# Last values after the last sums in the attention; the last image's 3x3 convolution by pairs of rows

## The chip, the cores and the metric

One core of a Trainium2 chip runs the whole program. The metric is the time of one execution on the device in microseconds, the median of several runs. All data are 32-bit floats.

## The reference

Four images of 128 channels and 64 x 64 pixels go through four layers. Each layer normalises its input by groups of channels, applies something, and adds the result to the input.

```python
# x: (4, 128, 64, 64)
x = x + attention(gn(x))      # layer 0: 4096 x 4096 scores for each image
x = x + conv5x5(gn(x))        # layer 1: weights built from radial tables
x = x + selective_scan(gn(x)) # layer 2: 64 + 64 channels, 64 states, both directions
x = x + conv3x3(gn(x)) + b    # layer 3

def attention(x):             # per image, n = 4096 pixels
    q, k, v = xt @ Wq.T + bq, xt @ Wk.T + bk, xt @ Wv.T + bv
    return softmax(q @ k.T * C ** -0.5) @ v

def conv2d(x, w, b):          # layer 3: 3x3, padding 1, with w of (128, 128, 3, 3)
    y = conv_general_dilated(x, w, (1, 1), [(1, 1), (1, 1)], ("NCHW", "OIHW", "NCHW"))
    return y + b[None, :, None, None]
```

## The kernel before, in words

The 128 channels lie on the 128 partitions, and the 4096 pixels of an image along the free dimension. TensorE (PE in the profile) works on blocks of 512 pixels (`MM`, one PSUM bank); the scan on chunks of 1024 (`CH`).

Two streams of work are written as Python generators and interleaved by hand, and the order in which they are emitted is the order in which each engine executes. One stream is `scan_core`, the recurrence of layer 2: 256 ticks for each image, in each of which GpSimd (POOL) multiplies `db<-dx,br` (L1082), ScalarE (ACT) makes decays `da` (L1075), VectorE (DVE) runs the recurrence (L1092) and part of the weighing (L1095), POOL the other part (L1113), and PE collects `y<-hc,sel` (L1127). The other stream, `images()`, is all the rest: for each image the attention, the 5x5 convolution and the operands of the scan (`front`), and later the end of layer 2 and the 3x3 convolution (`scan_end`, `back`). The scan of image b runs beside the front of image b+1. Every `yield` of the second stream states an estimate of its PE time (`PRODUCT` 0.86 us for a product of 512 columns, `HOP` 1.7 us), and after each half tick of the scan the program takes as many steps of the second stream as a credit of 2.8 us for a tick (`PACE`) allows; it is 1.5 us (`ENDPACE`) once no front is left. Before an image's first tick, `before(b)` takes steps of the second stream until the scan's operands of that image have been emitted. For image 0's front there is no scan yet, and after the last image's scan nothing but its own `scan_end` and `back` remains.

**The attention** of an image has 8 blocks of 512 queries, each with 32 tiles of 128 keys, so 256 units `u`. In unit u PE makes the scores (`sc`, L465), ACT the exponentials (`pt`, L471) into a ring of 8 slots, and PE adds `values(u - 2)` into the bank `acc` (L477). The sums of exponentials are made on PE from four ring slots at a time (`zp`, L499) in images 1 to 3. In image 0 (`fill`) DVE and POOL add them in `sided` and `sidep` (`side_sums`, L519). At the end of a block `evict` copies `zp` and `acc` out with ACT (`zs` L525, `raw` L527), `turn` turns the sums by tiny products (`pz`, L539), `invert` takes their reciprocals on DVE (L548, L550), `widen_out` spreads these with PE (`pzb`, L457), and `settle` multiplies and adds the residual on DVE (L562, L563). For blocks 0 to 6 these steps are spread over the next block's units. For block 7 they follow one another directly, after all of the block's values. Then the group norm of the 5x5 convolution waits for the last of the results.

**The 3x3 convolution** (`conv`, called from `back`) copies the normalised image into a padded tile `xpm` with ACT in four pieces (L370), and makes 8 blocks of 9 accumulated products each (`pcm`, L644). PE reads 32-bit floats in two records for each product in the trace, so 72 products are 144 records. For images 0 to 2 it runs beside the scan. For image 3 it is the last work of the program: DVE adds bias and residual straight from PSUM (L1278), and SP sends 256 KB to HBM (L1279). After it come the check of the range of the sums (`out_of_range`, L1396), its load into registers and a branch around a second, careful version of the program (`safe`), which is not taken with these inputs.

Of the kernel before, what the change touches and what calls it, by code (L numbers as in the profile page):

```python
# [24 lines left out]
F32 = mybir.dt.float32  # L25
# [27 lines left out]
def conv_preact_kernel(  # L53
# [170 lines left out]
    taps5 = cw[:, :NTAP, :]  # L224

    m3 = cw[:, : main_w.shape[1], :]
    kept = dram.tile([P, main_w.shape[1], C], F32, tag="kept", bufs=1, name="kept")

    def build_conv_weights(tmp):
        xx_sb = tmp.tile([P, NTAP, C], F32, name="xx_sb")  # L230
        nc.sync.dma_start(xx_sb, xhat)
        id_sb = tmp.tile([P, C], F32, name="id_sb")
        nc.sync.dma_start(id_sb, identity)
        picked = tmp.tile([P, 2, NTAP, C // 2], F32, name="picked")
        for n, (which, table, inds) in enumerate((("xx", wxx, indsxx), ("id", wid, indsid))):
            nr, oc = table.shape[1], table.shape[2]
            acc = picked[:, n]
            one = cw.rearrange("p k c -> p (k c)")[:, : NTAP * oc]
            one = one.rearrange("p (k o) -> p k o", o=oc)
            tab = tmp.tile([P, nr, oc], F32, name=f"tab{which}")  # L240
            nc.sync.dma_start(tab, table)
            ii = tmp.tile([P, NTAP], I32, name=f"ii{which}")
            nc.sync.dma_start(ii, inds.to_broadcast([P, NTAP]))
            fi = tmp.tile([P, NTAP], F32, name=f"fi{which}")
            nc.vector.tensor_copy(fi, ii)

            ng = tmp.tile([P, NTAP], F32, name=f"ng{which}")
            nc.vector.tensor_scalar(ng, fi, 0.0, float(nr), ALU.is_lt, ALU.mult)
            nc.vector.tensor_tensor(fi, fi, ng, ALU.add)
            nc.vector.tensor_scalar(fi, fi, 0.0, float(nr - 1), ALU.max, ALU.min)  # L250
            for r in range(nr):
# [26 lines left out]
        nc.sync.dma_start(kept, m3)  # L278

# [140 lines left out]
    def attention(b, xs, xn, v, st, safe, loads):  # L420
# [97 lines left out]
                s = sides[blk, e]  # L518
                eng.tensor_tensor(s, s, ring[:, u % NRING, :], ALU.add)  # L519

        def evict(blk):
# [47 lines left out]
        queries(0)  # L569
        ready.add((b, "begun"))  # L570
        yield HOP
        for u in range(N + 2):
            blk, j = divmod(u, NJT)
            cost = sums_due(u)
            if u < N:
                if safe and j == 0:
                    row_max(blk)
                scores(u)
                cost += PRODUCT
            w = u - 2  # L580
            if 0 <= w < N:
                values(w)
                cost += PRODUCT
# [8 lines left out]
                if d == NJT - 1:  # L592
                    evict(blk - 1)
                    if blk < NM:
                        for n, f in ((1, turn), (2, invert), (4, widen_out), (5, settle)):
                            after(u, n, f, blk - 1)
                    else:
                        turn(blk - 1)
                        invert(blk - 1)
                        yield PRODUCT  # L600
                        widen_out(blk - 1)
                        settle(blk - 1)
                        ready.add((b, "attended"))
                        break
            if j == 17 and blk + 1 < NM:
                queries(blk + 1)
                cost += PRODUCT
            for f, args in later.pop(u, ()):
                f(*args)
                cost += PRODUCT if f in (turn, widen_out) else 0.0  # L610
            next(loads, None)
            yield cost or HOP


    def conv(b, xs, tag, st, weights, k, finish, name, residual=False):
# [40 lines left out]
            done = i, acc  # L656
        yield HOP
        finish(*done)

# [539 lines left out]
    def program(safe):  # L1199
# [1 line left out]
        mats4, ynds, ends = {}, {}, {}  # L1201
        ready.clear()
        if safe:
            nc.sync.dma_start(m3, kept)

        def load(tile, b):
            for c in range(NCH):
# [15 lines left out]
        def front(b, xn, v):  # L1223
# [19 lines left out]
            if b + 1 < B:  # L1243
                return (yield from both(operands, start(b + 1, 10)))
            yield from operands

        def stage(b, pieces, done):

# [19 lines left out]
        def back(b):  # L1268
            xs, st, _ = ends[b]

            def put(i, acc):
                cut = bass.ts(i, MM)
                if b + 1 < B:
                    to = pools["bg"].tile([P, MM], F32, tag="w", bufs=4, name=f"o_{b}_{i}")
                    nc.scalar.activation(to, acc, AF.Identity, bias=col(MAINB))
                else:
                    to = xs[:, cut]
                    nc.vector.scalar_tensor_tensor(to, acc, col(MAINB), to, ALU.add, ALU.add)  # L1278
# [180 lines left out]
```

## Time and profile before

| | |
|---|---|
| median of 3 runs | 4513.8 us (4513.7, 4513.8, 4527.3) |
| profiled execution | 4519.1 us, of which the span on the engines is 4517.3 us |
| PE busy | 3996.2 us, 88% of the span |
| DVE busy | 3667.9 us, 81% |
| POOL busy | 3638.5 us, 81% |
| ACT busy | 2399.5 us, 53% |
| image 0's attention on PE | from 28 to 505 us |
| fronts of images 1, 2, 3 on PE | about 700 to 1670, 1660 to 2640, 2620 to 3580 us |
| last image's 3x3 convolution on PE | 4444.0 to 4508.7 us |

A busy share is an average over stages with different limits. PE is busy for 98 to 100 in each 100 us of the attentions that run beside a scan, and DVE and POOL are at 92 to 99 in the stage after 3700 us, where only the scan and short convolutions remain. At both ends of the program, image 0's front and the last convolution, one stream alone is running. Times in a view are counted from the start of the span.

### The profile page before, as it was taken

What the parts mean: (1) busy time and instruction counts of PE and PEld (TensorE: products, weight loads), DVE (VectorE), ACT (ScalarE), POOL (GpSimd) and SP (SyncE); (2) the same over time, 40 slices, a digit from 0 to 9 for tenths busy, and PEclk for the clock granted to TensorE, in tenths of its full rate; (3) what the DMA queues carried; (4) which work ended last, traced back from release to release, by engine and by line L of the source; (5) the groups of instructions that cost most, each with busy time, mean ns of one, the idle gap of its engine ahead of it and who ended that gap; (6) DMA issues with size and microseconds to landing.
All of it is one profiled execution on the core that took longest, in us unless ns stands there. A gap on an engine that the chain in (4) does not pass through costs nothing. (4 is left out here: it accounts for less than half of the span.)

```text
span 4517.3 us, 43608 instructions
## 1 busy us (share of the span) xinstructions
PE 3996.2 (88%) x13528; PEld 1482.2 (33%) x13528; DVE 3667.9 (81%) x3643; ACT 2399.5 (53%) x4420; POOL 3638.5 (81%) x1731
## 2 busy tenths in 40 slices
PE   8999998999999979999999879999999658575767
PEld 4444433333333323333333223333333112121212
DVE  4721217999998978999989879999999799999992
ACT  3333227666664476666654566666654654544441
POOL 3433308999998969999989789999999899999992
PEclk9999999999999989999999989999999878697888
DMA  1000016445444565455445555455445565656561
GB/s 63 6 1 1 5 60 229 171 168 180 170 175 157 174 218 196 172 179 174 174 154 177 188 209 176 162 176 177 175 161 182 211 226 203 233 193 231 184 233 48
DMA packets 210582, 719.51 MB, mean 159 GB/s; under 512 B 24864, under 2 KB 25760, under 8 KB 210208
## 3 DMA queue, kind: packets, MB, share of 16 engines
q1 hardware_dynamic: 208736, 715.87, 44.8%
q8 instruction: 109, 1.79, 0.2%
q14 instruction: 137, 1.12, 0.1%
q10 hardware_dynamic: 1600, 0.73, 0.1%
HBM read 649.07 MB, written 67.44 MB: 159 GB/s over the span
## 5 line engine op out<-in xcount | busy, mean ns | idle before, releaser
L1082 POOL TENSOR_TENSOR db<-dx,br 128x1024 f32<-128x1024 f32 x1024 | 2400.0, 2367 | 226.9 <-DMA dx<-dxd 76.7
L1075 ACT ACTIVATE da<-de,a_neg 128x512 f32<-128x512 f32 (+1 forms) x1795 | 1342.1, 751 | 736.0 <-DVE da L1092 444.5
L465 PE MATMUL sc<-r,x 128*128 128x512 f32 x2048 | 1082.5, 611 | 18.3 <-ACT r L434 12.4
L477 PE MATMUL acc<-pt,v 128*128 128x512 f32 x2048 | 1046.5, 593 | 1.6
L1113 POOL TENSOR_TENSOR hc<-hc,cr 128x1024 f32<-128x1024 f32 x406 | 960.1, 2365 | 17.6 <-ACT last L1108 15.1
L471 ACT ACTIVATE pt<-sc 128x512 f32<-128x512 f32 x1024 | 604.4, 590 | 572.4 <-PE sc L465 563.9
L1127 PE MATMUL y<-hc,sel 128*32 128x512 f32 x4096 | 654.2, 650 | 276.6 <-POOL hc L1113 273.5
L1095 DVE TENSOR_TENSOR hc<-da,cr 128x512 f32<-128x512 f32 (+1 forms) x1067 | 828.4, 776 | 68.8 <-issue 1.3
L1092 DVE TENSOR_TENSOR_SCAN da<-da,last,db 128x512 f32<-128x512 f32 (+1 forms) x464 | 728.1, 1569 | 24.1 <-POOL db L1082 17.6
L1092 DVE TENSOR_TENSOR_SCAN da<-da,da,db 128x512 f32<-128x512 f32 x449 | 577.9, 1287 | 14.3 <-ACT da L1075 13.4
L465 PEld LDWEIGHTS sc<-r,x 128*128 128x128 f32 x2048 | 359.1, 190 | 605.0 <-issue 378.4
L477 PEld LDWEIGHTS acc<-pt,v 128*128 128x128 f32 x2048 | 387.5, 190 | 497.2 <-issue 477.9
L1092 DVE TENSOR_TENSOR_SCAN hc<-da,hc,db 128x512 f32<-128x512 f32 x322 | 413.2, 1283 | 61.9 <-ACT da L1075 31.6
L1092 DVE TENSOR_TENSOR_SCAN hc<-da,last,db 128x512 f32<-128x512 f32 (+1 forms) x304 | 455.9, 1500 | 8.4 <-ACT da L1075 4.7
L519 POOL TENSOR_TENSOR sidep<-sidep,pt 128x512 f32<-128x512 f32 x120 | 170.5, 1421 | 279.9 <-ACT pt L471 277.8
L1127 PEld LDWEIGHTS y<-hc,sel 128*32 128x32 f32 x4096 | 94.1, 111 | 732.3 <-POOL hc L1113 363.6
L644 PE MATMUL pcm<-xpm,cw 128*128 128x512 f32 x576 | 291.2, 653 | 30.5 <-ACT xpm L370 30.5
L519 DVE TENSOR_TENSOR sided<-sided,pt 128x512 f32<-128x512 f32 x120 | 96.0, 800 | 227.5 <-ACT pt L471 226.1
L1092 DVE TENSOR_TENSOR_SCAN da<-da,db 128x512 f32<-128x512 f32 (+1 forms) x154 | 231.0, 1500 | 30.9 <-ACT da L1075 16.2
L808 PE MATMUL pe<-df,cw 128*128 128x512 f32 x560 | 255.2, 598 | 0.0
L499 PE MATMUL zp<-pt,ones 128*32 128x512 f32 x1536 | 202.4, 595 | 5.0 <-DVE xs L563 5.0
L1108 ACT COPY last<-da 128x1 f32<-128x1 f32 x469 | 73.1, 156 | 244.3 <-DVE hc L1095 242.5
(209 smaller groups left out, 2743.2 us busy)
## 6 DMA issues: line engine op xcount, KB each, us to landing
br<-bm SPq DMA_DIRECT2D x512, 512.0 KB, 5.2
cr<-cm SPq DMA_DIRECT2D x512, 512.0 KB, 3.9
de<-dd SPq DMA_DIRECT2D x64, 512.0 KB, 4.8
dx<-dxd SPq DMA_DIRECT2D x64, 512.0 KB, 6.2
x<-in_x_dram SPq DMA_DIRECT2D x16, 512.0 KB, 4.6
xs<-in_x_dram SPq DMA_DIRECT2D x16, 512.0 KB, 5.8
xsd<-xs SPq DMA_DIRECT2D x16, 512.0 KB, 5.2
xcd<-xc SPq DMA_DIRECT2D x16, 512.0 KB, 2.7
```

The lines of the kernel that those rows point to most:

```text
L465: nc.tensor.matmul(sc, xn[:, bass.ts(j, P)], rq[blk], start=True, stop=True)
L471: nc.scalar.activation(pt, sc, AF.Exp)
L477: nc.tensor.matmul(acc[blk], v[:, j, :], ring[:, u % NRING, :], start=j == 0, stop=j == NJT - 1)
L519: eng.tensor_tensor(s, s, ring[:, u % NRING, :], ALU.add)
L644: nc.tensor.matmul(acc.rearrange("p (r w) -> p r w", w=W), weights[:, t, :], xp[:, y : y + RPM, dx : dx + W], start=t == 0, stop=t == k * ...
L808: nc.tensor.matmul(flat(acc), cw[:, w * K5 + dx, :] if w < HSUM else more[:, w - HSUM, dx, :], view(r, dx), start=k == 1, stop=k == total ...
L1075: nc.scalar.activation(da, rep["de", b, c, d, g][:, bass.ts(h, size)], AF.Exp, scale=a_neg[:, at(i)])
L1082: nc.gpsimd.tensor_tensor(dbs[i], rep["dx", b, c, d, g], rows["b", b, c, d, q], ALU.mult)
L1092: nc.vector.tensor_tensor_scan(h, da, db[:, cut], before, ALU.mult, ALU.add)
L1095: nc.vector.tensor_tensor(hc[:, cut], h, rows["c", b, c, d, q][:, cut], ALU.mult)
L1113: nc.gpsimd.tensor_tensor(hcs[i], hcs[i], rows["c", b, c, d, q], ALU.mult)
L1127: nc.tensor.matmul(y[r : r + SG, :], sel, hcs[i - KG + 1 + gg][:, bass.ts(h, MM)], start=q == 0, stop=False, tile_position=(0, r), skip_gr ...
```

## The change

1. **Attention, last block of each image.** The values of the last four key tiles (`HELD`) are no longer issued inside the unit loop. After the loop come: values 252, what is pending of the sums, the last sums, the copy `zs` (images 1 to 3), values 253, `turn`, values 254, `invert`, values 255, `widen_out`, the copy `raw`, `settle`. `evict` is split in `evict_sums` and `evict`. In image 0 the last two side sums are issued right after the loop. The number of products is the same.
2. **3x3 convolution of the last image** (`conv_last`). Two output rows are made together from four input rows d0 to d3 and the three rows of weights w0 to w2. The four products are (w0 - w1 + w2)/2 on d2 - d1, (w0 + w1 + w2)/2 on d1 + d2, w0 on d0 - d2, and w2 on d3 - d1. The first output row is the sum of the first three, the second row is the second minus the first plus the fourth. Each of the four takes three products (dx = 1, 0, 2), so 12 for 1024 pixels where there were 18. POOL makes the two combinations with a minus sign on d1 (`cb` tiles from the scan's pool `hc`), DVE the other two. ACT copies the first product out, POOL adds it to and subtracts it from the residual rows, and DVE adds the other products and the bias. The tile `xpl` has no side columns; the outer dx products write 63 of the 64 columns.
3. **Banks.** Chunks 0 and 2 use the two double banks of the scan's decays (`da`); chunks 1 and 3 four single banks (`s`, `a`, `z`, `y`).
4. **Weights and output.** `last_weights` builds six combined rows of weights on DVE after the operands of image 3. The copy `kept` holds 15 taps instead of 9 (983 KB instead of 590 KB). The output leaves in 4 transfers of 512 KB instead of 8 of 256 KB.

```diff
+        def evict_sums(blk):
             zs = None
             if not fill:
                 zs = pools["bg"].tile([P, MM], F32, tag="zs", bufs=1, name=f"zs_{b}_{blk}")
                 nc.scalar.copy(zs, zp.pop(blk))
+            state[blk] = None, zs
+
+        def evict(blk):
             raw = pools["bg"].tile([P, MM], F32, tag="raw", bufs=1, name=f"raw_{b}_{blk}")
             nc.scalar.copy(raw, acc.pop(blk))
-            state[blk] = raw, zs
+            state[blk] = raw, state[blk][1]
...
-        for u in range(N + 2):
+        HELD = 4
+        for u in range(N):
...
-            if 0 <= w < N:
-                values(w)
-                cost += PRODUCT
+            if w >= 0:
+                if w < N - HELD:
+                    values(w)
+                    cost += PRODUCT
...
-                    if blk < NM:
-                        for n, f in ((1, turn), (2, invert), (4, widen_out), (5, settle)):
-                            after(u, n, f, blk - 1)
-                    else:
-                        turn(blk - 1)
-                        invert(blk - 1)
-                        yield PRODUCT
-                        widen_out(blk - 1)
-                        settle(blk - 1)
-                        ready.add((b, "attended"))
-                        break
+                    for n, f in ((1, turn), (2, invert), (4, widen_out), (5, settle)):
+                        after(u, n, f, blk - 1)
...
+        for w in (N - 2, N - 1) if fill else ():
+            side_sums(w)
+        blk = NM - 1
+        values(N - 4)
+        yield PRODUCT
+        while due:
+            sums(due.pop(0)[0])
+            yield PRODUCT
+        if not fill:
+            sums(N - 1)
+            yield PRODUCT
+        evict_sums(blk)
+        values(N - 3)
+        yield PRODUCT
+        turn(blk)
+        values(N - 2)
+        yield PRODUCT
+        invert(blk)
+        values(N - 1)
+        widen_out(blk)
+        evict(blk)
+        yield PRODUCT
+        settle(blk)
+        ready.add((b, "attended"))
...
+    def last_weights():
+        half, above = cw[:, LSUM : LSUM + 3, :], cw[:, LDIF : LDIF + 3, :]
+        nc.vector.tensor_tensor(half, m3[:, 0:3, :], m3[:, 6:9, :], ALU.add)
+        nc.vector.tensor_scalar(half, half, 0.5, None, ALU.mult)
+        nc.vector.scalar_tensor_tensor(above, m3[:, 3:6, :], -0.5, half, ALU.mult, ALU.add)
+        nc.vector.scalar_tensor_tensor(half, m3[:, 3:6, :], 0.5, half, ALU.mult, ALU.add)
+
+    def conv_last(b, xs, st, finish):
+        CK = CH // W // 2
...
+        def piece(c):
+            h0, h1 = 2 * CK * c + (c > 0), min(2 * CK * (c + 1) + 1, H)
+            normalise(rows[:, 1 + h0 : 1 + h1, :], xh[:, h0:h1, :], gn)
...
+        def combine(c):
+            d = [rows[:, 2 * CK * c + k : 2 * CK * (c + 1) + k - 1 : 2, :] for k in range(4)]
+            made = []
+            for eng, pairs in (
+                (nc.gpsimd, ((2, 1, ALU.subtract), (3, 1, ALU.subtract))),
+                (nc.vector, ((1, 2, ALU.add), (0, 2, ALU.subtract))),
+            ):
+                two = pools["hc"].tile([P, CH], F32, tag="hc", name=f"cb_{b}_{c}_{len(made)}")
+                for n, (i, j, op) in enumerate(pairs):
+                    made.append(flat(two[:, bass.ts(n, MM)]))
+                    eng.tensor_tensor(made[-1], d[i], d[j], op)
+            combined[c] = made
+
+        def banks_of(c):
+            if c % 2:
+                return [bank(tag, f"pl{tag}_{b}_{c}") for tag in "sazy"]
+            two = [
+                pools["wide"].tile([P, CH], F32, tag="da", bufs=2, name=f"pl{n}_{b}_{c}")
+                for n in range(2)
+            ]
+            return [t[:, bass.ts(h, MM)] for t in two for h in range(2)]
+
+        def products(acc, view, w):
+            for n, dx in enumerate((1, 0, 2)):
+                to = slice(max(1 - dx, 0), W - max(dx - 1, 0))
+                of_ = slice(max(dx - 1, 0), W - max(1 - dx, 0))
+                nc.tensor.matmul(
+                    flat(acc)[:, :, to], cw[:, w + dx, :], view[:, :, of_],
+                    start=n == 0, stop=n == 2, skip_group_check=True,
+                )
...
+        piece(0)
+        combine(0)
+        piece(1)
+        combine(1)
+        for c in range(NCH):
+            t_, o_, s_, e_ = banks_of(c)
+            diff, odd, total, even = combined.pop(c)
+            products(t_, diff, LDIF)
+            products(s_, total, LSUM)
+            products(e_, even, 0)
+            products(o_, odd, 6)
+            if c + 2 < NCH:
+                piece(c + 2)
+                combine(c + 2)
+            ts_ = pools["bg"].tile([P, MM], F32, tag="w", bufs=4, name=f"t_{b}_{c}")
+            nc.scalar.copy(ts_, t_)
+            nc.gpsimd.tensor_tensor(part(c, 0), part(c, 0), flat(ts_), ALU.add)
+            nc.gpsimd.tensor_tensor(part(c, 1), part(c, 1), flat(ts_), ALU.subtract)
+            for y, own in enumerate((e_, o_)):
+                nc.vector.scalar_tensor_tensor(
+                    part(c, y), flat(s_), col(MAINB), part(c, y), ALU.add, ALU.add
+                )
+            for y, own in enumerate((e_, o_)):
+                nc.vector.tensor_tensor(part(c, y), flat(own), part(c, y), ALU.add)
+            finish(c)
+            yield HOP
...
-            yield from conv(b, xs, "V", st, m3, 3, put, "m", residual=b + 1 < B)
+            if b + 1 < B:
+                yield from conv(b, xs, "V", st, m3, 3, put, "m", residual=True)
+            else:
+                yield from conv_last(
+                    b, xs, st,
+                    lambda c: nc.sync.dma_start(of[b][:, bass.ts(c, CH)], xs[:, bass.ts(c, CH)]),
+                )
```

More of the change, by code (lines that the diff above doesn't have):

```diff
@@ L226, in conv_preact_kernel @@
     m3 = cw[:, : main_w.shape[1], :]
-    kept = dram.tile([P, main_w.shape[1], C], F32, tag="kept", bufs=1, name="kept")
+    LSUM, LDIF, NKEPT = 9, 12, 15
+    kept = dram.tile([P, NKEPT, C], F32, tag="kept", bufs=1, name="kept")
     def build_conv_weights(tmp):
@@ L277, in build_conv_weights @@
             )
-        nc.sync.dma_start(kept, m3)
+        nc.sync.dma_start(kept, cw[:, :NKEPT, :])
     ASIZE, VSIZE = HP * (W + PAD) + PAD, (H + 2) * (W + 2) + PAD
@@ L519, in side_sums @@
                 eng.tensor_tensor(s, s, ring[:, u % NRING, :], ALU.add)
-        def evict(blk):
+        def evict_sums(blk):
             zs = None
@@ L571, in attention @@
         yield HOP
-        for u in range(N + 2):
+        HELD = 4
+        for u in range(N):
             blk, j = divmod(u, NJT)
             cost = sums_due(u)
[L575 to L578, printed above, removed]
-                cost += PRODUCT
+            if safe and j == 0:
+                row_max(blk)
+            scores(u)
+            cost += PRODUCT
             w = u - 2
-            if 0 <= w < N:
-                values(w)
-                cost += PRODUCT
+            if w >= 0:
+                if w < N - HELD:
+                    values(w)
+                    cost += PRODUCT
                 d = w % NJT
@@ L592, in attention @@
                 if d == NJT - 1:
+                    evict_sums(blk - 1)
                     evict(blk - 1)
-                    if blk < NM:
-                        for n, f in ((1, turn), (2, invert), (4, widen_out), (5, settle)):
-                            after(u, n, f, blk - 1)
-                    else:
-                        turn(blk - 1)
-                        invert(blk - 1)
-                        yield PRODUCT
-                        widen_out(blk - 1)
-                        settle(blk - 1)
-                        ready.add((b, "attended"))
-                        break
+                    for n, f in ((1, turn), (2, invert), (4, widen_out), (5, settle)):
+                        after(u, n, f, blk - 1)
             if j == 17 and blk + 1 < NM:
@@ L658, in conv, with flat, part @@
         finish(*done)
+    def last_weights():
[6 more added lines that the diff above has]
+        CK = CH // W // 2
+        xp = pools["big"].tile([P, VSIZE], F32, tag="V", name=f"xpl_{b}")
+        rows = xp[:, : (H + 2) * W].rearrange("p (h w) -> p h w", w=W)
+        nc.gpsimd.memset(rows[:, 0, :], 0.0)
+        nc.gpsimd.memset(rows[:, H + 1, :], 0.0)
+        gn = yield from group_norm(st, f"m{b}")
+        xh = xs.rearrange("p (h w) -> p h w", w=W)
+        def flat(t):
+            return t.rearrange("p (h w) -> p h w", w=W)
+        def piece(c):
+            h0, h1 = 2 * CK * c + (c > 0), min(2 * CK * (c + 1) + 1, H)
+            normalise(rows[:, 1 + h0 : 1 + h1, :], xh[:, h0:h1, :], gn)
+        combined = {}
+        def combine(c):
[26 more added lines that the diff above has]
+                )
+        def part(c, y):
+            return xs[:, bass.ts(c, CH)].rearrange("p (h t w) -> p h t w", t=2, w=W)[:, :, y, :]
+        piece(0)
[24 more added lines that the diff above has]
+            yield HOP
@@ L1203, in program @@
         if safe:
-            nc.sync.dma_start(m3, kept)
+            nc.sync.dma_start(cw[:, :NKEPT, :], kept)
         def load(tile, b):
@@ L1245, in front @@
             yield from operands
+            last_weights()
         def stage(b, pieces, done):
@@ L1272, in put @@
                 cut = bass.ts(i, MM)
[L1273 to L1278, printed above, removed]
-                nc.sync.dma_start(of[b][:, cut], to)
-            yield from conv(b, xs, "V", st, m3, 3, put, "m", residual=b + 1 < B)
+                to = pools["bg"].tile([P, MM], F32, tag="w", bufs=4, name=f"o_{b}_{i}")
+                nc.scalar.activation(to, acc, AF.Identity, bias=col(MAINB))
+                nc.sync.dma_start(of[b][:, cut], to)
+            if b + 1 < B:
[5 more added lines that the diff above has]
+                )
         def both(*gens):
```

## The prediction

> **What bounds the kernel now.** I read the page's slices first, then the chain that ended last in order of time, then the timelines around the places of the change. The slices, 113 us each:
>
> ```profile
> PE   8999998999999979999999879999999658575767
> ...
> DVE  4721217999998978999989879999999799999992
> ACT  3333227666664476666654566666654654544441
> POOL 3433308999998969999989789999999899999992
> ```
>
> There are three regimes: image 0's front (slices 1 to 5), where PE alone is full; the scans beside a front, where PE, DVE and POOL are all near full; and from slice 33 the scan alone, bound by DVE and POOL. The last slice is a fourth, and the chain says what sets its length:
>
> ```profile
> 4442.70 1.25 ACT xpm L370
> 4443.95 0.04 issue
> 4444.00 64.67 PE pcm L644 x144
> 4508.66 0.02 issue
> 4508.69 0.75 DVE xt L1278
> 4509.44 0.07 DVE out_of_range L1396
> ```
>
> The reader should see that 64.67 us on PE lie bare on the path, with nothing before or beside them that could take their place. The timeline shows how PE paces itself there:
>
> ```profile
> 4444.00 6.28 PE L644 MATMUL pcm<-xpm,cw 128*128 128x512 f32 x8 [6.86 <-ACT xpm L370]
> 4445.01 0.34 PEld L644 LDWEIGHTS pcm<-xpm,cw 128*128 128x128 f32 x1 [0.52 <-issue]
> ...
> 4450.12 0.19 PEld L644 LDWEIGHTS pcm<-xpm,cw 128*128 128x128 f32 x1 [0.24 <-issue]
> 4450.55 0.19 PEld L644 LDWEIGHTS pcm<-xpm,cw 128*128 128x128 f32 x1 [0.24 <-issue]
> ```
>
> At first the loads come every 0.86 us (0.34 + 0.52), later every 0.43 us (0.19 + 0.24). One load is one record and two records are one product of 512 columns, so a product costs 0.858 us. The 144 records at 0.429 are 61.8 us; the slow start costs the other 2.9.
>
> **What the Trainium skill says.** "TensorE: Matmul & The Clock Gate", Part 1, says that PE runs at half rate after an idle window and gets its full rate after about 3.4 us of activity. The trace agrees on the factor of two; here the slow phase lasts some 5 us, after 6.86 us idle. "SBUF — State Buffer", section "SBUF: two separate sides", says that a DVE operation with two SBUF inputs and a POOL operation lock each other out. The trace agrees: in image 0 a POOL difference of 528 columns takes 1.62 us where DVE makes its combinations at the same time, and 1.09 to 1.11 us otherwise; the DVE row spans 0.70 to 1.63.
>
> ```profile
> L705 POOL TENSOR_TENSOR df<-xpe x16: 1093/1108/1620, 513.1 to 3408.2; 128x528 f32<-128x528 f32 x12, 128x594 f32<-128x594 f32 x4
> L731 DVE TENSOR_TENSOR combos<-xpe x12: 697/705/1634, 513.0 to 569.3; 128x528 f32<-128x528 f32 x12
> L823 POOL TENSOR_TENSOR xs<-xs,q x8: 1262/1266/1269, 525.2 to 616.6; 128x512 f32<-128x512 f32 x8
> L830 DVE TENSOR_TENSOR xs<-xs,pm x8: 680/684/689, 528.9 to 619.7; 128x512 f32<-128x512 f32 x8
> ```
>
> **The last convolution.** PE: 48 products instead of 72. Of these 16 have 512 columns (16 x 0.858 = 13.7 us) and 32 have 504 (32 x 0.845 = 27.0). With the same slow start of 2.9 that is 43.6 us, 21.0 less than 64.67.
>
> Start: the first product needs not only the normalised rows but a POOL difference of them. ACT's first piece has 17 rows instead of 16 (1.25 x 17/16 = 1.33, +0.08), and the POOL difference costs 1.62 x 512/528 = 1.57 plus 0.05 for the handover: PE starts 1.7 us later, at 4445.7. If POOL and DVE don't collide it is 1.2; if POOL's two inputs have to wait for both DVE combinations (0.68 each) it is 2.7. The second and third operand are then ready: three products at the slow rate last 5.1 us.
>
> Middle: one chunk takes PE 10.2 us. Beside it DVE makes two combinations (1.25 each when colliding: image 0's first six take 7.48 us in the timeline) and four additions (two at 0.75, two at 0.68), 5.4 us. POOL does four operations of 1.27 to 1.6, at most 6.4. ACT has 1.25 + 0.58 us. The combinations of chunk c+2 stand in each queue ahead of the evictions of chunk c, and chunk c+1 is ready before PE asks for it. In chunks 0 and 2 two products share a double bank, so evictions may have to wait for the other half; the next use of that tile is a whole chunk (10 us) later, and the work of about 6 us fits. I take zero for the middle. If that cover were too short, each chunk could lose what the evictions exceed 10.2 by, none by these numbers.
>
> End: in the last chunk, with single banks, the copy (0.58), two POOL operations (2.5) and the two DVE additions of the sum (1.5) run while PE makes the other nine products (7.6 us), with 2 to 3 us to spare. After the last product one DVE addition of 0.68 remains where 0.75 was. The program's end, 7.8 us from `out_of_range` to the end of the span, hides the transfer. Before, 256 KB landed 2.0 us after issue; transfers of 512 KB in the page's last section take 2.7 to 6.2, and up to about 5 is hidden. I take zero, at worst +1.
>
> Sum: 4445.7 + 43.6 + 0.03 + 0.68 + 0.07 = 4490.1 against 4509.5: **-19.4 us**, between -20.9 and -16.4 with the bounds above and 1 us more or less of slow start.
>
> **`last_weights`.** Four DVE operations of 384 columns, by scaling from 512 (0.68 and 0.75): 0.5 + 0.3 + 0.55 + 0.55 = 1.9 us. They stand after the first few ticks of image 3's scan, where DVE waits for POOL:
>
> ```profile
> 3603.34 1.28 DVE L1092 TENSOR_TENSOR_SCAN hc<-da,hc,db 128x512 f32<-128x512 f32 x1
> 3610.01 2.30 DVE L1092 TENSOR_TENSOR_SCAN da<-da,db 128x1024 f32<-128x1024 f32 x1 [5.39 <-POOL db L1082]
> ```
>
> That gap covers them, so +0.3, between 0 and +1.9 without it. The weights' transfer was issued long before. The larger `kept` transfer (393 KB more) goes out in image 0, where the DMA share is 0.02 or less; zero.
>
> **The attention, image 0.** Its end lies bare:
>
> ```profile
> 499.28 2.74 PE L477 MATMUL acc<-pt,v 128*128 128x512 f32 x6
> ...
> 500.28 1.26 POOL L519 TENSOR_TENSOR sidep<-sidep,pt 128x512 f32<-128x512 f32 x1 [2.17 <-ACT pt L471]
> ...
> 503.74 0.16 DVE L548 COPY zall<-pz 128x4 f32<-128x4 f32 x1 [4.65 <-PE pz L539]
> ...
> 504.26 1.13 PE L457 MATMUL pzb<-ident,zr 128*128 128x128 f32 x8 [0.56 <-DVE zr L550]
> 505.49 0.70 DVE L562 TENSOR_TENSOR pzb<-raw,pzb 128x512 f32<-128x512 f32 x1 [1.38 <-PE pzb L457]
> ```
>
> Before, PE waits once after the last scores: 0.56 us for the reciprocals, in front of `pzb`. The new order fills this wait with values 254 and 255. But the scores of unit 255 move only one product forward, to 497.57; their exponentials end near 499.3 and POOL's last side sum near 500.7, while PE reaches `turn` already at 500.15, after values 253. So PE waits 0.55 us there. The work is the same, one wait is exchanged for another: 0, within 0.6 either way. `raw` (0.59) now follows the last value, but runs beside `pzb` (1.13).
>
> **Images 1 to 3.** At image 1's end PE waits 0.91 us for `zs` and DVE 1.66 us for `pz`; values 253 to 255 cover part of this. Against it the tail has one more step in the credit (0.86 us), so the front falls back by about a third of a tick, which a scan that waits for its operands at the boundary gets back. In the orders of the two programs the fronts of images 1 to 3 shift by one to six products' time against the scan and meet again. I take -0.5 an image, -1.5 together, between -6 and +8: a shifted transfer can cost (POOL waited up to 11.1 us for a `br`) or spare that.
>
> **Sum:** -19.4 + 0.3 + 0 - 1.5 = -20.6. The profiled execution of 4519.1 would become 4498.5. Two of the three runs shown are at 4513.7 and 4513.8, 5.3 below the profiled one, so the median goes to **4493 us**.
>
> **Rivals.** *The evictions set the pace* (chance 0.07): if lockouts between DVE and POOL double their operations, POOL's four take 6.4 and DVE's six near 10 us, as long as PE's chunk; with the dependences in a chunk some 3 us are lost in each of four. The gain falls to 8, 4506 us. For it speaks the row of 1.6 us; against it that PE's 10.2 us leave room even then. *The shifted order costs* (0.08): two waits like the 11.1 us one, less 20, give some 4508 us. For it speaks that PE, DVE and POOL are all near full beside a front; against it that the shift returns to zero.
>
> *PE stays at the half rate* (0.06, slower): each record then costs 0.86 instead of 0.43 us. If the four groups of three products were separated by waits that keep PE in its slow state, all 96 records would take 82 us instead of the 43.6, so 38 more than forecast, and the program 4531 us. From 45 more slow records on the gain is gone, from some 76 it is slower by over 0.3%. The slow start of this very loop speaks for it; against it, every operand but the first is ready early, so the stream should not break.
>
> **How the numbers follow.** 0.3%, about what a measurement can tell from no change, is 13.5 us: faster means below 4500.3. The likeliest case has 0.79 and lies between 4483 and 4500; both rivals with a partial gain end within 0.3% (0.15); the third is slower (0.06). The range goes from 4483 to 4508, with the bounds of the middle stages at both ends, and leaves the third rival out.
>
> **What would show it.** In the new profile: 96 records of the last convolution in 43 to 45 us without waits inside; the first about 1.7 us after the rows; a last DVE addition and then 7.8 us of ending; `pz` in image 0 some 1.1 us earlier but the first `pq` at about 514.2 again; the last convolution's start moved by under 8 us. A stream broken between groups, an end over 8.5 us after the last product, or a later start of the last convolution than at 4452 would make the prediction wrong.

## The result and the profile after

| | before | after |
|---|---|---|
| median, 5 runs each, run by turns | 4519.4 us (4513.7 to 4527.3) | 4491.1 us (4487.9 to 4495.8) |
| profiled execution | 4519.1 us, span 4517.3 | 4493.8 us, span 4491.9 |

The changed kernel is faster: the ratio is 0.9939, with a 95% interval from 0.9925 to 0.9954. That is some 28 us of 4519.

I read the slices of the page of after first, the same rows as before:

```profile
PE   8999998999999979999999879999999748576676
...
DVE  4722217999999978999999879999999799999996
ACT  3333227666665476666664566666654644444533
POOL 3433308999999969999999889999999799999995
```

The regimes are the same. Only the last slice moves by more than one digit: 2 became 6 for DVE and 5 for POOL, and 1 became 3 for ACT, since the slice that held the bare convolution is now partly scan and partly combinations and additions beside PE. The chain that ended last, in order of time (start, length, engine, tile and line), shows the new end:

```profile
4439.24 1.79 POOL cb L724
4441.03 0.04 issue
4441.08 12.23 PE pl L741 x24
...
4463.50 10.19 PE pl L741 x24
...
4481.34 2.56 PE pla L741 x6
4483.90 0.02 issue
4483.92 0.69 DVE xt L772
4484.61 0.07 DVE out_of_range L1515
```

PE takes 4441.08 to 4483.90, 42.8 us, for 96 records, and no other engine appears inside. The first 24 cost 12.23 us and a later 24 cost 10.19: the slow start is 2.0 us. Now, however, a POOL row of 1.79 us stands ahead of PE. The timeline at that place and the summary of the tile `cb` tell why:

```profile
4439.20 9.06 DVE L724 TENSOR_TENSOR cb<-xpl 128x512 f32<-128x512 f32 x6 [2.26 <-ACT xpl L372]
4439.24 10.14 POOL L724 TENSOR_TENSOR cb<-xpl 128x512 f32<-128x512 f32 x6 [1.40 <-ACT xpl L372]
```

```profile
L724 DVE TENSOR_TENSOR cb<-xpl x8: 692/1748/1760, 4439.2 to 4459.4; 128x512 f32<-128x512 f32 x8
L724 POOL TENSOR_TENSOR cb<-xpl x8: 1282/1710/1777, 4439.2 to 4457.7; 128x512 f32<-128x512 f32 x8
```

Columns of the second fence are minimum, median and maximum in ns. Both engines make their combinations at once and both are slow: DVE 1.75 us instead of 0.69, POOL 1.71 instead of 1.28. That fits the exclusion of DVE and POOL that the prediction named. It costs PE's start some 0.5 us once (1.79 us for the first POOL combination instead of 1.28); the middle of the convolution has room for it.

The end stretch, from the end of the last `po` product to the start of `out_of_range`, measures 72.2 us before and 52.2 after, so **20.0** of the 25.3 us between the two profiled executions lie there. The other 5 lie elsewhere, and were found with the following cut: the starts of POOL's `db` products, one for each tick of the scan, cut the program into the same pieces in every kernel. Ticks 0 to 505 take 1881.4 us before and 1876.1 after, ticks 505 to 520 (the passage from image 1's scan to image 2's) 104.6 and 99.0, ticks 520 to 1023 1748.6 and 1752.7. So something that is none of the convolution's gave 5.6 us at a single place. The cut does not begin at zero: the first tick starts at 687.3 us in before and 689.5 in after (688.8 to 693.0 in all the kernels that follow); where these 2.2 us come from was not isolated.

### The profile page after: what moved, and what is told of

The parts are those of the page before. It is cut to its first block, busy times and chain, and to the rows that moved or that the text cites. A ratio compares the mean times of both kernels' runs of the same rounds, so it can differ in the third digit from the quotient of the medians.

```text
span 4491.9 us, 43563 instructions
## 1 busy us (share of the span) xinstructions
PE 3980.9 (89%) x13480; PEld 1472.6 (33%) x13480; DVE 3689.8 (82%) x3665; ACT 2403.6 (54%) x4425; POOL 3662.0 (82%) x1745
## 5 line engine op out<-in xcount | busy, mean ns | idle before, releaser
L666 PE MATMUL pcm<-xpm,cw 128*128 128x512 f32 x432 | 226.3, 668 | 15.1 <-ACT xpm L372 15.1
```

What stands on the lines that cost most here:

```text
L666: nc.tensor.matmul(acc.rearrange("p (r w) -> p r w", w=W), weights[:, t, :], xp[:, y : y + RPM, dx : dx + W], start=t == 0, stop=t == k * ...
```

## The experiments

**The two parts apart.** `e1_conv_only` has the new last convolution, and the attention as before. `e2_attention_only` has the attention's new order and nothing else. `e3_again` is the whole change once more, from the same text. `e4_both_ends` adds two small edits to the whole change: image 0 keeps its last four values ahead of `turn`, and the first chunk of the convolution starts with the product whose operand DVE makes.

```diff
# e4_both_ends, image 0 only
+            for w in range(N - HELD, N):
+                values(w)
+                yield PRODUCT
+            evict_sums(blk)
+            evict(blk)
+            turn(blk)
+            invert(blk)
+            widen_out(blk)
# e4_both_ends, conv_last
-            products(t_, diff, LDIF)
-            products(s_, total, LSUM)
+            first = ((t_, diff, LDIF), (s_, total, LSUM))
+            for args in first[::-1] if c == 0 else first:
+                products(*args)
```

> The convolution alone, the attention as before. Theory (nearly all of the gain is in the last convolution, about 20 us between the last product of scan_end and the last addition on DVE; the rest is wander of the middle stages): 19 to 21 us faster than before, ratio 0.9955, the same stretch of 52.3 us from the last po product to out_of_range as with the whole change. Rival (the attention of images 1 to 3 brings 6 us or more): as above in the stretch, and the whole change is then faster than this kernel by 5 us or more in the timed runs.

> The attention alone, the last convolution as before. Theory: within 3 us of the time before; in image 0 the first product of the 5x5 convolution comes 1.5 us later against the scores than before, because values 254 and 255 run at the half rate after the tiny products of turn; images 1 to 3 give back 0 to 3. Rival (the new order in images 1 to 3 brings what the whole change shows ahead of the last convolution): 5 to 8 us faster than before, and the ticks of images 2 and 3 come 5 to 9 us earlier in the trace, as with the whole change.

> The whole change once more, unaltered, for a second trace. Theory (the middle stages wander from run to run): the ticks of images 2 and 3 move by several us against the first trace of the same program, the last convolution and image 0's end agree with the first trace within 0.3 us; about 0.994 of the time before. Rival (the earlier ticks come from the order): the ticks agree with the first trace within 2 us everywhere.

> The whole change with two edits: in image 0 the four held values come before turn (images 1 to 3 as in the change), and in chunk 0 of the last convolution the product of DVE's sum comes before the product of POOL's difference. Theory: image 0's first product of the 5x5 convolution comes 1.3 to 1.7 us earlier against the scores (values at 0.43 us a record again), and PE starts the last convolution about 1.1 us earlier after the normalised rows (0.7 for DVE's first sum in place of POOL's 1.8); together 2.5 us less than the whole change, under what five rounds resolve with certainty but visible in the trace. Rival for the start (DVE and POOL lock each other out, and DVE is the loser when POOL goes first): the first sum takes 1.5 to 1.8 as well, and the start moves by less than 0.3.

| | median us | ratio to before | 95% interval | end stretch us |
|---|---|---|---|---|
| convolution alone | 4502.1 | 0.9966 | 0.9953 to 0.9979 | 52.2 |
| attention alone | 4512.2 | 0.9982 | 0.9975 to 0.9988 | 72.4 |
| whole change again | 4492.4 | 0.9941 | 0.9928 to 0.9953 | 52.5 |
| both ends | 4490.3 | 0.9936 | 0.9923 to 0.9948 | 51.7 |

Within the intervals the parts add up: 0.34% and 0.18% make 0.52%, the whole 0.59%. The convolution's 20.0 us appear only where the convolution is new. The attention edit is worth about 8 us alone and 9.7 on top of the convolution, where the prediction had 1.5 and my expectation for the second kernel at most 3. Its gain sits at the same place in all kernels that have it: tick 512 starts 14.8 us earlier in after, 17.6 in the attention alone, 15.1 in the repeat, and 0.1 us *later* in the convolution alone. The two traces of the whole change agree within 0.7 us from tick 505 to tick 520 and differ by 4.5 us at tick 1023: the early ticks belong to the program, while the stage after them wanders. In the fourth kernel the edit at the convolution does what was expected (PE's wait ahead of it is 7.63 us instead of 8.76); the one in image 0 doesn't, as shown below. Its time can't be told from the repeat's.

**Image 0's end, and the double banks.** `e6_turn_first` puts all four values of image 0 behind `turn`. `e5_last_double` turns the choice of banks round, so that the last chunk lies in double banks.

```diff
# e5_last_double, banks_of
-            if c % 2:
+            if c % 2 == 0:
# e6_turn_first, image 0 only
+            evict_sums(blk)
+            turn(blk)
+            invert(blk)
+            for w in range(N - HELD, N):
+                values(w)
```

> The whole change with the banks exchanged: chunks 0 and 2 of the last convolution in single banks, chunks 1 and 3 in the double ones. Theory (in a double bank the copy of the first product waits for the fourth, which lies in the same tile): in the last chunk the copy starts after the last product, and then come the copy 0.6, two POOL operations of 1.27 and DVE's additions 0.75 + 0.68 + 0.68: 4 to 5.5 us from the last product to out_of_range instead of 0.65. Rival (the halves are waited for singly): 0.65 as in the change.

> The whole change with image 0's turn ahead of all four held values (images 1 to 3 as in the change). Theory (PE drops to its half rate in or after the tiny products of turn and needs a few us of full work to leave it, and where that falls varies from run to run): of the eight records of the four values some or all take 0.86 us instead of 0.43, the first product of the 5x5 convolution comes 18 to 22 us after the exponential of unit 253 (18.1 before). Rival (what slows them is a neighbour: ACT or DVE reading beside): the slow records fall together with an operation of ACT or DVE, and end with it.

With the double banks at the end one run took 4497.5 us. The timeline of its last microseconds:

```profile
4484.65 0.58 ACT L764 COPY t<-pl 128x512 f32<-128x512 f32 x1 [17.25 <-PE pl L741]
...
4485.31 1.26 POOL L765 TENSOR_TENSOR xt<-xt,t 128x512 f32<-128x512 f32 x1 [15.34 <-ACT t L764]
4486.53 1.26 POOL L766 TENSOR_TENSOR xt<-xt,t 128x512 f32<-128x512 f32 x1
...
4488.49 1.28 DVE L772 TENSOR_TENSOR xt<-pl,xt 128x512 f32<-128x512 f32 x2
```

ACT's copy of the *first* product starts only after the last one (17.25 us idle, ended by PE), because the fourth product lies in the same double tile. So copy, two POOL operations and the DVE additions, which in after run beside PE, follow PE one after another: 5.2 us from the last product to the last addition, where after needs 0.7. This is the cover that the prediction counted on for its last chunk. I had expected to read it at `out_of_range`, and that was wrong: here this check runs at 4484.77 us, ahead of the additions, and part of the program's end with it, so the program itself ends only 3.6 us later than after does, both counted from the end of the last `po` product.

For image 0, I measured from the start of ACT's exponential of unit 253 to the first product `pq` of the 5x5 convolution: 18.14 us before, 18.15 with the convolution alone, 19.62 after, 19.62 with the attention alone, 17.94 in the repeat, and 21.35 with all four values behind `turn` (one run of 4493.2 us). Two executions of the same text differ by 1.7 us. With all four values ahead of `turn` (`e4_both_ends`) it is 19.1, where 1.3 to 1.7 us less than in after was expected. PE's rows behind the tiny products `pz` in their timelines, after first, then the repeat, then the kernel with `turn` first:

```profile
501.64 0.36 PE L544 MATMUL pz<-ones,sidep 128*128 128x1 f32 x2
501.87 3.37 PE L479 MATMUL acc<-pt,v 128*128 128x512 f32 x4
505.03 1.38 PE L459 MATMUL pzb<-ident,zr 128*128 128x128 f32 x8
```

```profile
503.15 0.36 PE L544 MATMUL pz<-ones,sidep 128*128 128x1 f32 x2
503.38 1.96 PE L479 MATMUL acc<-pt,v 128*128 128x512 f32 x4
505.18 1.05 PE L459 MATMUL pzb<-ident,zr 128*128 128x128 f32 x8
```

```profile
502.01 0.36 PE L544 MATMUL pz<-ones,sidep 128*128 128x1 f32 x2
502.24 5.38 PE L479 MATMUL acc<-pt,v 128*128 128x512 f32 x8
```

The same four records take 3.37 us in one execution and 1.96 in another. PE doesn't wait there; it runs at half rate, just after 16 products of a single column that take 2 us together. The clock that the trace records as granted says the same: from 502 to 505 us its mean is 0.55 of full speed in after and 1.00 in the repeat. With eight records behind `turn`, about five are slow (clock 0.60). With none behind it, in `e4_both_ends`, `pzb` takes 2.05 us instead of the 1.13 of before, and that is the whole 0.9 us by which `pq` is later than before. The Trainium skill, "TensorE: Matmul & The Clock Gate", Part 1, says that the monitor of PE's activity works in a window that runs freely of the program, so that the slow phase falls differently from run to run. The two executions of one text agree with that; that the tiny products are what sets it off fits all these rows, but it was not isolated.

**What gives 10 us at image 2?** The first theory was SP's queue: in before the loads of `br` and `cr` for ticks 512 and 513 stand behind a store that waits for half a tick's work. `e7_early_load` moves the loads of an image's first tick ahead of that half tick, on `e1_conv_only`. The rival was the extra step of credit that the attention's new tail has (one `yield PRODUCT` more), which shifts all that follows. `e8_step_fewer` is the whole change with the first of the new yields taken out.

```diff
# e7_early_load, scan_core (on e1_conv_only)
+            early = i > 0 and (i + AHEAD) % TICKS == 0
+            if early:
+                do(load, i + AHEAD)
             yield i
             do(decay, i + 1, 1)
-            do(load, i + AHEAD)
+            if not early:
+                do(load, i + AHEAD)
# e8_step_fewer, the attention's tail
         values(N - 4)
-        yield PRODUCT
```

> The convolution alone with the attention as before, and one more edit in the scan: the loads of an image's first tick are issued half a tick earlier. In SP's order this moves one thing: de, dx, br and cr of image 2's first tick come ahead of the store cm<-bs of block 5, as in the whole change, and no longer behind it. Theory (SP's queue gives what the attention edit seemed to give): the ticks from 512 on come 7 to 11 us earlier against the convolution alone, and the time is 6 to 10 us less than its 4502, about that of the whole change. Rival (the saved waits of PE and DVE at the attentions' ends give it): no more than 2 us from the convolution alone.

> The whole change without one of its new yields (values 252 and the step after it count as one), so that the order of the products in the attention stays the new one while SP's order at image 2's first tick is that of before: the store cm<-bs of block 5 ahead of the loads. Theory (SP's queue): tick 512 comes 8 to 12 us later than in the whole change, and the time is 6 to 10 us above it, near 4500. Rival (the saved waits of PE and DVE): within 2 us of the whole change, and tick 512 early as there.

The early load gives 4502.2 us (0.9961, 0.9947 to 0.9974), the same as the 4502.1 without it: tick 512 alone comes earlier, by 4.4 us, and tick 513 is past by 1.3 us later than without the edit. With one step fewer the whole change also takes 4502.1 us (0.9963, 0.9949 to 0.9976), and tick 512 is back within 0.4 us of before. This second result alone would have fitted the queue as well, since the store stands ahead of the loads again; the first one speaks against the queue. So the attention's new *order* of products gives nothing by itself; the step count does.

**The step alone.** `e9_one_more_step` has the old order of the attention and one yield more. `e10_early_two` moves the loads (and second decays) of an image's first two ticks, so that the early tick 512 isn't followed by a late 513. `e12_no_three` came from looking at DVE at that place; it leaves out three small group-norm products of the last attention.

```diff
# e9_one_more_step (on e1_conv_only)
                         turn(blk - 1)
+                        yield PRODUCT
                         invert(blk - 1)
# e10_early_two (on e1_conv_only)
+            early = i > 0 and (i + AHEAD) % TICKS < KG
+            if early:
+                do(decay, i + 1, 1)
+                do(load, i + AHEAD)
             yield i
...
# e12_no_three (on e1_conv_only), group_norm
+        short = name == "a3"
+        if not short:
             nc.vector.tensor_tensor(means, means, mean, ALU.add)
             nc.vector.tensor_tensor(means, means, means, ALU.mult)
             nc.vector.tensor_tensor(means, means, vars_, ...)
-        nc.vector.tensor_reduce(total, means, AX.X, ALU.add)
+        nc.vector.tensor_reduce(total, vars_ if short else means, AX.X, ALU.add)
...
```

> The new last convolution with the old order of the attention's products, and one more step of credit between the turn and the reciprocal at the attention's end, so that all that follows in the order of rounds stands one step later, as it does in the changed kernel. Theory (the 9 to 10 us of the attention edit come from this one step alone, by where it puts the start of image 2's scan): the first tick of image 2 comes 10 to 15 us earlier than in the kernel with only the convolution changed, the three small group-norm products beside it take 0.2 us each instead of 1.2, 2.3 and 2.3, and the time is 4490 to 4495 us. Rival (the new order of the values is needed for it): the first tick of image 2 stays within 2 us and the time is 4500 to 4504 us.

> The new last convolution with the old attention, and the loads for the first two ticks of an image issued ahead of the half step that precedes them (the loads of the first tick alone brought nothing). Theory of the queue (at image 2's start SP holds the loads of two ticks behind a store that waits for the end of a half step, and that is the 9 to 10 us): both ticks come 6 to 9 us earlier and the time is 4493 to 4497 us. Rival (the loss lies on VectorE, where the small products of the last attention's group norm wait for POOL, 1.2 + 2.3 + 2.3 us instead of 0.6, and the scans behind them wait too): the three products stay long, ticks 512 and 513 are past within 2 us of before, and the time is 4500 to 4504 us.

> The new last convolution with the old attention, and in the last image's attention the group norm leaves out the part of the variance that lies between the channels of a group: its three small VectorE products (1.2 + 2.3 + 2.3 us in the kernel before, at 2601.3 us) are not issued, all else stays. Theory of the shared port (these three hold up the scan behind them, and with it the first tick of image 2): VectorE's scan behind the group norm starts 5 to 6 us earlier, tick 512 comes 4 to 6 us earlier, and the time is 4496 to 4499 us against 4502. Rival (SP's order alone sets that tick, VectorE has slack there): the tick moves by less than 2 us and the time is 4500 to 4504 us. If the rival waits elsewhere on VectorE, for instance for POOL's next product, part of the 5 us is given back within four ticks.

One line, the extra yield, takes the convolution-only kernel from 4502.1 to **4490.9 us** (0.9945, 0.9932 to 0.9959), the time of the whole change; tick 512 comes 17.6 us earlier than in the kernel with the convolution alone, more than the 10 to 15 expected. The early loads of two ticks give nothing (4505.8 us; 0.9972, 0.9960 to 0.9983): tick 512 is 8.7 us earlier than with the convolution alone, but at tick 516 only 2.0 us are left of it. Without the three small products the time is 4497.0 us (0.9954, 0.9940 to 0.9968), as the theory of the shared port had it. These medians come from sets in which before itself lay between 4518.3 and 4521.4 us, and the intervals of 0.9966 and 0.9954 overlap, so it is the traces that carry a gain of this size. Here are DVE's rows in the timeline of before at that place, and POOL's beside them:

```profile
2601.11 0.18 DVE L352 TENSOR_SCALAR gn_work<-gn_sums 128x32 f32<-128x32 f32 x1
2601.32 1.18 DVE L354 TENSOR_TENSOR gn_work<-gn_work 128x32 f32<-128x32 f32 x1
2602.53 2.26 DVE L355 TENSOR_TENSOR gn_work<-gn_work 128x32 f32<-128x32 f32 x1
2604.83 2.26 DVE L356 TENSOR_TENSOR gn_work<-gn_work 128x32 f32<-128x32 f32 x1
...
2607.73 1.24 DVE L1092 TENSOR_TENSOR_SCAN hc<-da,last,db 128x512 f32<-128x512 f32 x1
```

```profile
2599.97 2.48 POOL L944 TENSOR_TENSOR delta<-delta,u 128x512 f32<-128x512 f32 x2
2602.41 4.63 POOL L949 TENSOR_TENSOR xc<-delta,xc 128x1024 f32<-128x1024 f32 x2
```

An operation on 32 columns takes 2.26 us, as long as one POOL product of 1024 columns (4.63 / 2 = 2.32), and ends when that one ends. Elsewhere the same operation is 0.19 us, so I read the rest as a wait for the port. In the trace DVE works through its queue in order, so the scan of the tick at 2607.73 stands behind all three, and ACT's next decay behind that scan. ACT's rows show it, before first, then the kernel without the three products:

```profile
2609.01 0.69 ACT L1075 ACTIVATE da<-de,a_neg 128x512 f32<-128x512 f32 x1 [8.06 <-DVE hc L1092]
```

```profile
2605.15 0.69 ACT L1174 ACTIVATE da<-de,a_neg 128x512 f32<-128x512 f32 x1 [3.03 <-DVE hc L1191]
```

The timeline of after has one tick's scan ahead of the group norm, and only one small operation meets POOL:

```profile
2599.15 1.28 DVE L1208 TENSOR_TENSOR_SCAN hc<-da,last,db 128x512 f32<-128x512 f32 x1
...
2603.27 1.20 DVE L354 TENSOR_SCALAR gn_work<-gn_sums 128x32 f32<-128x32 f32 x1
2604.51 0.19 DVE L356 TENSOR_TENSOR gn_work<-gn_work 128x32 f32<-128x32 f32 x1
2604.73 0.19 DVE L357 TENSOR_TENSOR gn_work<-gn_work 128x32 f32<-128x32 f32 x1
```

The scan behind the group norm in the kernel without the three products starts at 2603.87 us, against 2608.91 in its parent: 5.0 us, the price of the three (5.7) less what one other operation now waits (0.9). The Trainium skill, "SBUF — State Buffer", section "SBUF: two separate sides", calls the shared pair of ports an exclusive lock that is held for a whole instruction, not a division of bandwidth. The trace agrees, and shows the consequence: the price of being locked out is what is left of the *other* engine's instruction, here up to 2.26 us, whatever the size of one's own.

**Are there two parts in a row?** After this, 6 us were still missing between 4497.0 and 4490.9. `e13_both` joins the early loads of two ticks and the missing three products, in case the queue's wait shows only once DVE's is gone.

> The two preceding edits together, on the new last convolution with the old attention: the last attention's group norm without its three small VectorE products (the between-channel part of its variance is left out), and the loads of an image's first two ticks ahead of the half step. Alone they gave 5 us and nothing. Theory (the boundary at image 2 has two parts in a row, VectorE behind POOL and then the loads behind SP's store, and the second shows only when the first is gone): ticks 512 to 520 come 8 to 10 us earlier than in the kernel with only the convolution changed, and the time is 4490 to 4494 us, as with the extra step. Rival (the loads bring nothing with or without the three products; what is left lies in the order of the engines' own work): ticks 513 to 520 are 3 to 5 us earlier and the time is 4496 to 4500 us.

It takes 4497.35 us (0.9954, 0.9941 to 0.9968). The loads give nothing here either; the rival holds. The cut by ticks then shows where the 6 us are. Lengths in us from the profiled executions:

| kernel | ticks 0 to 505 | 505 to 520 | 520 to 1023 | three small products |
|---|---|---|---|---|
| before | 1881.4 | 104.6 | 1748.6 | 1.2, 2.3, 2.3 |
| convolution alone | 1879.2 | 105.3 | 1749.6 | 1.2, 2.3, 2.3 |
| one early load | 1882.9 | 105.2 | 1749.9 | 1.2, 2.3, 2.3 |
| two early loads | 1880.1 | 104.2 | 1752.9 | 1.2, 2.3, 2.3 |
| whole change, one step fewer | 1878.2 | 104.7 | 1752.3 | 1.2, 2.3, 2.3 |
| three products left out | 1879.3 | 99.9 | 1752.1 | none |
| left out, and two early loads | 1882.0 | 99.1 | 1750.0 | none |
| after | 1876.1 | 99.0 | 1752.7 | 0.2, 0.2, 0.2 |
| whole change again | 1875.3 | 98.6 | 1748.9 | 0.2, 0.2, 0.2 |
| after, double banks last | 1876.4 | 98.7 | 1751.3 | 0.2, 0.2, 0.2 |
| after, `turn` first | 1872.9 | 98.8 | 1751.0 | 0.2, 0.2, 0.2 |
| attention alone | 1872.4 | 98.8 | 1752.6 | 0.2, 0.2, 0.2 |
| both ends | 1873.1 | 98.7 | 1755.4 | 0.2, 0.2, 0.2 |
| old order, one step more | 1872.9 | 98.7 | 1752.6 | 0.2, 0.2, 0.2 |

The passage at image 2 takes 104.2 to 105.3 us wherever DVE's three products are long, and 98.6 to 99.9 wherever they are short or absent. **That settles 5 to 6 us**: they are the wait of these three products, since leaving them out is enough to bring the short passage, and SP's order, which I had suspected first, has no part in them. That the wait is the port lock is the reading of the rows above. Another 6 us come before tick 505: 1872 to 1876 us in the kernels with the extra step, 1878 to 1883 in those without it. They come in pieces (2.5 us over ticks 202 to 206 in after, for one), and which waits they were was not isolated. After tick 520 a text differs from itself by 3.8 us (1752.7 and 1748.9), so nothing can be said of differences of that size there.

## Why the prediction was right, and where it was not

The forecast was 4493 us, faster at 0.79; the median is 4491.1. The mechanism is the one given as the likeliest, and its main term is right. Three smaller terms were mis-sized, and one correction had no ground. That the number came within 2 us is luck in part: counted from the five-run median of before, 4519.4, the change gave 28.3 us where 20.6 had been worked out, and the forecast started some 5 us too low.

- **The last convolution, -19.4: right, measured -20.0.** The start moved by 1.9 us (6.86 to 8.76 of PE's wait) where 1.7 was worked out. PE took 42.8 us where 43.6 was; the difference is the slow start, 2.0 us instead of 2.9. After the last product 0.65 us pass to `out_of_range`, where 0.68 + 0.07 was counted. The ending is 7.2 us where 7.8 was, so it hides the larger transfer. The 24-record pieces of the chain have no wait inside, which excludes both the rival in which the evictions set the pace and the one in which PE stays at half rate.
- **The cover of the last chunk: right.** With the double banks at the end it is gone, and 5.2 us follow the last product, as shown above.
- **`last_weights`, 1.9 us of work in a gap, +0.3: the size was wrong, and without the attention edit the loss too.** The timeline of after has the four operations in a row:

```profile
3597.10 1.70 DVE L690 TENSOR_TENSOR cw<-cw 128x384 f32<-128x384 f32 x1
3598.83 1.31 DVE L691 TENSOR_SCALAR cw<-cw 128x384 f32<-128x384 f32 x1
3600.18 1.50 DVE L692 SCALAR_TENSOR_TENSOR cw<-cw 128x384 f32<-128x384 f32 x1
3601.71 2.58 DVE L693 SCALAR_TENSOR_TENSOR cw<-cw 128x384 f32<-128x384 f32 x1
```

  They take 7.1 us, not 1.9; the scaling from the number of columns left out the lock, beside POOL's long instructions. In after no loss is visible: ticks 772 to 780, where they stand, take 29.3 us against 29.9 with the attention alone, which hasn't got them. With the convolution alone the four take 8.5 us, and ticks 772 to 780 take 30.0 us against 25.4 before, more than the 1.9 that the prediction allowed; at tick 1023 3.4 us of this are left. All six kernels with the new convolution and without the extra step show it (30.0 to 30.3). It is a reading of the traces: no run took these operations out alone.
- **Image 0, 0 within 0.6: +1.5 in after, -0.2 in the repeat.** `pz` did come earlier: counted from the exponential of unit 253 its last pair starts after 6.0 us instead of 7.2, close to the 1.1 stated. But `pq` started at 515.27 instead of 514.25, and in two more kernels with this order it came 1.4 us late as well. The step that failed is "one wait is exchanged for another": the order puts two values behind the tiny products, where PE can be at half rate, and they then cost 0.79 us a record instead of 0.43, with 1.38 us for `pzb` instead of 1.13.
- **Images 1 to 3, -1.5 between -6 and +8: mis-sized, about -10, outside its own range** (4492.4 against 4502.1 us with and without the attention edit). The prediction named the extra step in the credit and took it for a small cost that returns. It is the cause of nearly all of the attention's gain (5 to 6 us of it at image 2, the rest not isolated), and the reordering that the prediction priced is worth nothing measurable (one step fewer: 4502.1 us). What the prediction had in view as the possible spared wait was a transfer, `br`; the runs with early loads show that the wait for `br` was only what came last, and the one without the three products that 5 us of it went on DVE.
- **From the profiled execution to the median, -5.3: no ground.** Three runs were too few. In the later sets the medians of before are 4518.3 to 4521.4, so the profiled execution of 4519.1 was a typical one and the correction should have been about zero. The sum made against it, 4498.5, is to be held against the profiled 4493.8: 4.7 us too little gain. The two errors cancelled.

## What to carry to other kernels

Cost the bare stretch at the end by its own rows: that term was right to 0.6 us of 20, and it carried the result. Where two streams are interleaved by a credit, a step more or less is a change of its own, and its effect may be larger than that of the edit it came with; try the step alone before the edit is given the credit. Small DVE operations on a path that the scan shares should not be emitted where POOL has long instructions queued: here their price was POOL's instruction (2.26 us), not their own size (0.19).

## What the runs showed of the hardware that was not expected

- A DVE operation of 32 columns took 2.26 us beside a POOL product of 1024 columns, and 0.19 us elsewhere: three of them cost the program 5 to 6 us.
- After 16 one-column products PE ran at half rate for up to about five records of 512 columns (3.37 us for four instead of 1.96, at a granted clock of 0.55 instead of 1.00), in one execution of a text and not in another.
- A copy that needs one half of a double tile in PSUM, written early, waited for the product in the other half: 17.25 us idle on ACT, and 5.2 us from the last product to the last addition instead of 0.7.
